# Block 3's first keys with their ones from DRAM, and batch 1's routing ahead of the first maxima, in a perceiver on one Trainium2 core

## The chip, the cores and the metric

The kernel runs on one core of one Trainium2 chip. The metric is the device time of one execution in microseconds, the median of several runs. Its engines are TensorE (PE for the products, PEld for the loading of its weights), VectorE (DVE), ScalarE (ACT), GpSimd (POOL) and SyncE (SP), which issues all DMAs of this kernel. Each engine works through its own instructions in their order; an instruction waits until the semaphores it names have been raised.

## What is computed

Two batches of 256 tokens of width 256 go through four blocks. Each block attends to a context of 4096 tokens (`xattn`), then to itself (`attn`), and ends with a feed-forward layer (`ffn`). What the change touches lies in blocks 2 and 3 (shortened from the reference):

```
x = x + L2_attn(layernorm(x))            # 16 heads
x = x + L2_ffn(layernorm(x))             # router over 8 experts, the best two
                                         # weighted, plus one shared expert
x = x + L3_xattn(layernorm(x), ctx, mask)  # 16 heads of 16, 4096 keys
x = x + L3_attn(...); x = x + L3_ffn(...)
```

In `L2_ffn` the logits of the router go to eight experts; the two largest get the gates softmax(v1, v2), all others zero. In `L3_xattn` scores are q·k / 4 plus a large negative number where the mask drops a key, then softmax over the 4096 keys, then the values.

## The kernel before

**Lanes and order.** Two lanes of work, `a` and `x`, share the engines, each with its own pools. The program is written in stages; a scheduler at build time then fixes the order of instructions on each engine from its own estimate of durations. Only what is chained by hand (`tie` for TensorE's instructions in block 3's exponents, `behind` for one instruction after another) is not free for it to move. All DMAs are on one queue, SP's, and use eight semaphores in turn: a DMA is issued only when the eighth before it has landed.

**Block 2, end.** The two batches are staggered: while batch 0's `l2_ffn` runs on lane a, batch 1's cross-attention and then `l2_attn(1)` run on lane x. `l2_attn` writes its queries to DRAM and loads them back as stacked tiles (`stack`, L526; the last of these loads is a `rows_from`). Its result is added at L1234. `l2_ffn(1)` follows on lane a: layernorm (statistics L426 and L427, a 128x2 step on VectorE L432, the power on GpSimd L417, `axn` L441), four transposes (L449), the plain copy `xf` (L468), logits (L1073, bias L1078), two rounds of `first_max` (L1089 to L1097) and some small steps that give the gates `g8` (to L1262). `along` (L1107 on) transposes the gates (L1111), halves them into `grow` (L1113), writes the 8 rows to DRAM and loads them back spread over 128 partitions (L1115, L1119). Then come the shared expert and four pairs of experts, each by `glu`: 12 + 12 products (L413), tanh on ACT (L1028), L1032, the gate on GpSimd (L1134), u (L1132 or L1135), and the split of u into a high part (ACT, L404) and a low part (VectorE, L407). Weights are split in the same way: loaded as `awr` (L340), high part `aw` on ACT (L404), low part on GpSimd (L406) or VectorE (L407). The sum x is written at L1269.

**Block 3's cross-attention.** `l3_xattn` is a generator for both batches. Its work is cut into 32 places: 2 batches x 4 groups of 4 heads x 4 pieces of 1024 keys. For each place there are two passes. `max_steps` loads the key tile (two DMAs from `akh_d`, one from `akl_d`, L1370; the mask row L1371, 16 KB) and, at a group's first piece, the query tile (six DMAs of 16 rows, L526), multiplies (L1378, two products of 64x512) and takes maxima (L1380, 128x1024 to 128x2, eight a place). `exponents` multiplies again with keys as the stationary side (L1407), takes exponentials (ACT, L1411; L1409 in the last places, where they are wide) and multiplies with the values (L581). The maxima run five places ahead of the exponents (`ahead`), so 40 reduces and one more come before the first exponent; afterwards one reduce stands beside each step of exponents. There are seven key tiles in a ring and three query tiles. A key tile holds, beside the three rows of each key element, a row of ones in which the first is the mask; `x3_tiles` fills each of the seven tiles with ones on GpSimd (L1300) and copies `unmask` into each of the three query tiles (L1296, GpSimd too). `later` holds steps that are due a number of exponent steps from now.

**Queries of block 3.** `x3_queries(b, x)` is a layernorm, transposes, a product with `x3.wq` and a write to `q_d` (L521). In `af` it follows `l2_ffn(b)`. For batch 1 its products use the PSUM banks ("mm" of lane a) which the first exponents need as score banks.

**Masks.** `masks`, in block 1, writes the mask numbers `md` and `mk_d` and a small tensor of ones, `fill_d`.

In the profile, `xf<-xk,xq` are the products for the maxima, `xpm<-xf` the reduces, `amm` or `xs<-xq,xk` the score products, `xp` the exponentials, `axn` the layernorm's output on lane a, `aqT` the queries of block 3.

Of the kernel before, what the change touches and what calls it, by code (L numbers as in the profile page):

```python
# [18 lines left out]
F32 = mybir.dt.float32  # L19
F32R = mybir.dt.float32r  # L20
# [8 lines left out]
P = 128  # L29
# [261 lines left out]
class Lane:  # L291
# [231 lines left out]
    def rows_from(self, x, at, n, src, step=1):  # L523

        to = x[at : at + step * (n - 1) + 1 : step].bitcast(F32)
        self.nc.sync.dma_start(to, src.bitcast(F32) if src.dtype == F32R else src)  # L526

# [116 lines left out]
class Perceiver:  # L644
# [461 lines left out]
    def along(self, fp, g):  # L1106
# [13 lines left out]
        return out  # L1120

    def glu(self, fp, h, wg, wu, xT, m, gate=None):


        k, nc = self.a, self.nc
        psg = k.proj_t(wg, xT, m)
        g = k.t(fp, [P, 2, S], "g")
        self.tanh_half(g, psg)
        psu = k.proj_t(wu, xT, m)
        u = k.t(fp, [P, 2, S], "u")  # L1130
        if gate is None:
            nc.vector.scalar_tensor_tensor(u, psu, 0.5, g, ALU.mult, ALU.mult)  # L1132
        else:
            nc.gpsimd.tensor_tensor(g, g, gate, ALU.mult)  # L1134
            nc.vector.tensor_mul(u, psu, g)  # L1135
        k.split(h, u)
# [36 lines left out]
    def l2_attn(self, k, b, x):  # L1173
# [3 lines left out]
        with k.pool("a2", bufs=1) as ap:  # L1177
# [37 lines left out]
            for g in range(4):  # L1215
                k4, q4 = ks[g % 2], qs[g % 2]
                g4 = slice(GRP * g, GRP * g + GRP)
                k.stack(k4, q_d, g4, k.KEYS)
                k.stack(q4, q_d, g4, k.QUERIES)
                k.rows_from(q4, k.ADD, 2, sqd[:, g4, :])  # L1220
                k.rows_from(k4, k.ADD + 2, 2, sqd[:, g4, :])
                acc = k.mm()
                ps = [k.mh_scores(ap, lambda j: k4[:, j, t * P : (t + 1) * P], lambda j: q4[:, j, :], 0.5) for t in range(2)]
                for t in range(2):
                    k.mh_values(ps[t], lambda j: v[:, t, 4 * g + j, :], acc, t == 0, t == 1)
                k.mh_finish(g, acc, o)()
# [10 lines left out]
    def l2_ffn(self, b, x):  # L1237
# [4 lines left out]
        with k.pool("f2", bufs=2) as fp:  # L1242
            br = k.row("f2.br", fp)
            xf = k.t(fp, [P, 2, S], "xf", bufs=1)
            xnT = k.transposed(k.layernorm(x, fp), fp, "xnT", plain=xf)
            lg = self.logits(k, xf, "f2.gate", bias=br)
            v1, hot1 = self.first_max(lg, "a")
            v2, hot2 = self.first_max(self.without(lg, hot1), "b")
# [13 lines left out]
            nc.vector.tensor_add(g8, g8, h2)  # L1262
            gates = self.along(fp, g8)
            h = k.t2(fp, [P, 10, S], "h", bufs=1)
            self.glu(fp, h[:, 0:2, :], s1, s3, xnT, 0)
            for e in range(0, 8, 2):
# [17 lines left out]
    def x3_tiles(self, at):  # L1284
# [8 lines left out]
        if c == 0 and i < self.Q_SETS:  # L1293

            x = tile(f"q{i}", S)
            nc.gpsimd.tensor_copy(x, self.unmask.unsqueeze(1).to_broadcast([P, GRP, S]))  # L1296
            self.x3_q.append(x)
        if at < self.RING:
            x = tile(f"k{at}", 512)
            nc.gpsimd.memset(x.bitcast(F32), 1.0)  # L1300
            self.x3_k.append(x)
        return self.x3_q[i % self.Q_SETS], self.x3_k[at % self.RING]
# [10 lines left out]
    def masks(self):  # L1313

        k, nc = self.a, self.nc
        with k.pool("mask", bufs=1) as mp:
# [10 lines left out]
            nc.sync.dma_start(self.fill_d, fill)  # L1327

    def x3_queries(self, b, x):

        k = self.a
        (wq,) = k.weights("x3.wq")
        with k.pool("x3q", bufs=1) as ap:
            xnT = k.transposed(k.layernorm(x, ap), ap, "xnT")
            k.to_dram(k.proj_t_split(wq, xnT, ap, "qT", bias="x3.bq"), self.q_d[b])

    def l3_xattn(self, xs):
# [8 lines left out]
        def place(at):  # L1346
# [3 lines left out]
            return b, g, c, i  # L1350

        def max_steps(at):


            b, g, c, i = place(at)
            g4 = slice(GRP * g, GRP * g + GRP)
            q4, k4 = self.x3_tiles(at)
            if c == 0:
                for h in range(2):
                    at = h * self.HALF  # L1360
                    for r, part in enumerate(k.QUERIES):
                        src = self.q_d[b, part].rearrange("m (h d) n -> d (m h) n", d=HD)
                        k.rows_from(q4, at + r, HD, src[:, g4, :], self.PARTS)
                    if i >= self.Q_SETS:
                        k.rows_from(q4, at + self.SHIFT, 2, self.zeros, self.PARTS)
                state[i] = q4, k.t(self.early, [P, 2, GRP, 2 * n_c], "pm", bufs=2), []
            q4, pm, ks = state[i]
            u2 = slice(2 * c, 2 * c + 2)
            for r, src in ((0, self.kh_d), (1, self.kh_d), (2, self.kl_d)):
                nc.sync.dma_start(k4[r :: self.PARTS].bitcast(F32), src[b, u2, :, g4, :].rearrange("u d j n -> (u d) j n"))  # L1370
            nc.sync.dma_start(k4[self.MASK :: self.HALF].bitcast(F32), self.mk_d[b, u2])  # L1371
            ks.append(k4)
            for j in range(GRP):
                for t in range(2):
                    both = self.x3_find()
                    for h in range(2):
                        rows = slice(h * self.HALF, (h + 1) * self.HALF)
                        tie(nc.tensor.matmul(both[:, h * 512 : (h + 1) * 512], lhsT=q4[rows, j, t * P : (t + 1) * P], rhs=k4[rows, j, :], start=True, stop=True))  # L1378
                    at = pm[:, t, j, 2 * c : 2 * c + 2]
# [82 lines left out]
        self.zeros = k.t(self.early, [2 * GRP, S], "zeros", F32R, bufs=1)  # L1462
        nc.gpsimd.memset(self.zeros.bitcast(F32), 0.0)
        xp = self.late
        self.x3_banks(k)
# [5 lines left out]
        yield 1, None  # L1471
        for at in range(ahead):
            steps = max_steps(at)
            advance(self.STEPS)
# [3 lines left out]
        self.tied = None  # L1478
        tie = self.tie
        for at in range(n):  # L1480
            steps = max_steps(at + ahead) if at + ahead < n else iter(())
            for s in range(4):
# [355 lines left out]
    def run(self):  # L1838
# [14 lines left out]
        nc.vector.tensor_mul(self.w12, self.w1h, a.col("f0.w2", 0, 8))  # L1853
        self.q_d = a.dram([B, 2, 2, P, S], "q_d")

# [4 lines left out]
        self.mk_d = a.dram([B, L // 512, GRP, 512], "mk_d")  # L1860
        self.v_d = a.dram([B, 4, P, L // 512, 4 * GRP * (HD + 1)], "v_d")
        self.md = a.dram([B, L], "md")

        self.fill_d = a.dram([4, 2048], "fill_d")
        
        def af(n, b):
# [3 lines left out]
            else:  # L1870
                xb[b] = self.l2_ffn(b, xb[b])
                self.x3_queries(b, xb[b])

        a.p_bufs = 2
        x.p_bufs, x.score_tags = 4, [(x, "s")]
        with ExitStack() as wa:
            a.wraw = wa.enter_context(a.pool("wraw", bufs=2))
            a.wp = wa.enter_context(a.pool("w", bufs=4))
            with ExitStack() as early:
# [3 lines left out]
                with self.psum(x, mm=2, s=2, pr=1), self.psum(a, mm=3), x.pool("wraw", bufs=1) as x.wraw, x.pool("w", bufs=2) as wp, x.pool("xq", bufs=1) as self.xq:  # L1883
# [17 lines left out]
                    with x.pool("x", bufs=1) as xp:  # L1901
# [4 lines left out]
                        for n in range(1, 3):  # L1906
# [5 lines left out]
                            if n == 2:  # L1912
                                self.early = early.enter_context(a.pool("x3e", bufs=2))
                            xb[1] = self.xattn(xp, n, 1, xb[1], xq[1])
                            self.prep_alone(xp, *self.ALONE.get((n, 1), (0, ())))
                            if n < 2:
# [3 lines left out]
                    x.mm_tags = ["mm", "mm", "pr"]  # L1920
                    xb[1] = self.l2_attn(x, 1, xb[1])
                x.p_bufs = 3
                with ExitStack() as self.x3_psum, self.psum(a, mm=2, acc=1), x.pool("x3", bufs=2) as self.late:
# [50 lines left out]
```

## Time and profile before

| | |
|---|---|
| median of 3 runs | 1514.52 us (1509.82, 1514.52, 1514.57) |
| the profiled execution | 1513.83 us |
| its span, first to last instruction | 1512.1 us |
| granted TensorE clock, mean over the span | 0.94 |
| busy in the span: PE, DVE, ACT, POOL | 89%, 73%, 59%, 34% |
| end of `l2_attn(1)`: x of batch 1 written | 863.8 us |
| first maximum (L1380) begins | 870.44 us |
| gates transposed and halved (`grow`) | 904.03 us |
| `l2_ffn(1)` writes x (L1269) | 940.84 us |
| first score products of the exponents flow | 954.92 us |
| last maximum ends | about 1231.5 us |
| last value products of block 3's cross-attention | 1275.5 us |
| PE busy in 850–900, 980–1000 us | 30.19 of 50, 19.82 of 20 |

Times in the profile are microseconds from the start of the span. A timeline's line gives the start, the length, the engine, the line of the program, the operation, the output and inputs, and in brackets the idle time before it and what ended it. A group's line gives the busy time and the mean length in ns of one instruction, and after the bar the idle time just before them. "PEclk" or "clock" is the share of TensorE's full clock that was granted.

### The profile page before, as it was taken

Reading aid. Unit: us, or ns where it says so; the run is one execution under the profiler, and the core shown is the slowest. Engines: PE = TensorE matmul, PEld = TensorE weight load, DVE = VectorE, ACT = ScalarE, POOL = GpSimd, SP = SyncE. Lnnn points to the kernel's source line nnn. Section 1 sums busy time; section 2 is a strip of 40 time slices with the busy share of each in tenths; the row PEclk is TensorE's granted clock in tenths of the full one; section 3 lists DMA queues with packets and bytes.
Section 4 is the critical chain, followed back from the end, with each engine's and each line's share of the span. In section 5 each row is a group of like instructions: output and inputs, shape, how many; then the busy total and the mean of one; then the engine's idle time right before and its main releaser. Section 6 shows DMA issues by size and latency. Waiting matters only on the chain.

```text
span 1512.1 us, 29306 instructions
## 1 busy us (share of the span) xinstructions
PE 1353.1 (89%) x11278; PEld 1108.8 (73%) x11278; DVE 1108.8 (73%) x1863; ACT 891.4 (59%) x1644; POOL 521.0 (34%) x397
## 2 busy tenths in 40 slices
PE   7898788979998999998998767899999998987698
PEld 6898778969998998998898436455555544774588
DVE  6999855446467878885588599799999961566675
ACT  6676555637775655764664303688888897233243
POOL 6755344335445544664335413000000001531130
PEclk9999999979999999999999959899999999986799
DMA  8754164556455556445642542333333312300262
GB/s 288 250 152 131 33 190 161 184 172 217 149 177 169 176 177 214 146 155 179 164 128 89 172 165 95 121 119 109 126 122 107 113 53 61 136 1 30 84 218 75
DMA packets 125143, 212.00 MB, mean 140 GB/s; under 512 B 12840, under 2 KB 89240, under 8 KB 121480
## 3 DMA queue, kind: packets, MB, share of 16 engines
q1 hardware_dynamic: 125004, 210.13, 44.1%
q8 instruction: 89, 1.46, 0.4%
q14 instruction: 50, 0.41, 0.1%
HBM read 181.32 MB, written 28.61 MB: 139 GB/s over the span
## 4 chain that ended last, share of the span: by engine, by line
PE 48%; DVE 14%; ACT 5%; DMA 4%; POOL 4%; issue 3%; SPq 1%; POOLq 0%; DVEq 0%; ACTq 0%
PE amm L413 9%; PE xacc L581 7%; PE xmm L413 6%; PE xf L1378 5%; DVE xpm L1380 4%; PE xs L413 4%; PE xpr L413 4%; DMA awr<-in_w 2%; PE amm L1407 2%; POOL aw L406 2%; ACT xp L1409 1%; PE xmm L788 1%; PE amm L1796 1%; PE xs L1407 1%; PE amm L581 1%
## 5 line engine op out<-in xcount | busy, mean ns | idle before, releaser
L1380 DVE TENSOR_REDUCE xpm<-xf 128x2 f32<-128x1024 f32 x256 | 310.2, 1234 | 7.5 <-PE xf L1378 5.9
L1411 ACT ACTIVATE xp<-amm 128x512 f32<-128x512 f32 x284 | 162.0, 595 | 29.6 <-PE amm L1407 17.6
L406 POOL TENSOR_TENSOR aw<-awr,aw 128x1024 fp32r<-128x1024 f32 (+1 forms) x53 | 126.5, 2389 | 148.2 <-ACT aw L404 114.8
L404 ACT CAST aw<-awr 128x1024 fp32r<-128x1024 f32 (+1 forms) x112 | 114.0, 1021 | 99.8 <-DMA awr<-in_w 60.3
L413 PE MATMUL xmm<-xvx,xpT 128*128 128x256 f32 x1152 | 167.2, 291 | 2.8 <-DVE xo L801 1.3
L581 PE MATMUL xacc<-xp,xv 128*17 128x256 f32 x2048 | 161.0, 387 | 4.1 <-DVE xot L1430 1.1
L413 PE MATMUL xs<-xkx,xqkT 128*128 128x256 f32 x1152 | 162.1, 285 | 2.7 <-POOL xkx L738 1.9
L738 POOL TENSOR_TENSOR xvx<-xraw,xvx 128x512 fp32r<-128x512 f32 x96 | 131.9, 1389 | 89.6 <-ACT xvx L736 89.1
L1378 PE MATMUL xf<-xk,xq 64*128 64x512 f32 x512 | 135.8, 527 | 22.2 <-DVE xpm L1380 13.6
L413 PEld LDWEIGHTS xmm<-xvx,xpT 128*128 128x128 f32 x1152 | 147.9, 193 | 6.0 <-DVE xo L804 2.0
L413 PEld LDWEIGHTS xs<-xkx,xqkT 128*128 128x128 f32 x1152 | 147.6, 191 | 4.6 <-POOL xkx L738 2.1
L1378 PEld LDWEIGHTS xf<-xk,xq 64*128 64x128 f32 x512 | 51.1, 196 | 124.1 <-issue 83.2
L407 DVE TENSOR_TENSOR aw<-awr,aw 128x1024 fp32r<-128x1024 f32 (+1 forms) x59 | 86.6, 1473 | 60.9 <-ACT aw L404 60.8
L1445 POOL TENSOR_TENSOR ax<-xou,xmh_ri 128x128 f32<-128x128 f32 x8 | 3.2, 402 | 315.9 <-DVE xmh_ri L1441 315.9
L413 PE MATMUL amm<-axnT,aw 128*128 128x256 f32 x636 | 98.9, 313 | 10.2 <-ACT axnT L404 5.5
L413 PE MATMUL amm<-ah,aw 128*128 128x256 f32 x768 | 99.6, 286 | 6.0 <-ACT au L1013 2.9
L413 PEld LDWEIGHTS amm<-axnT,aw 128*128 128x128 f32 x636 | 91.3, 217 | 17.8 <-ACT axnT L404 7.2
L413 PEld LDWEIGHTS amm<-ah,aw 128*128 128x128 f32 x768 | 94.7, 191 | 8.7 <-POOL aw L406 3.7
L738 POOL TENSOR_TENSOR xkx<-xraw,xkx 128x512 fp32r<-128x512 f32 x48 | 72.1, 1503 | 82.9 <-ACT xkx L736 82.3
L1411 ACT ACTIVATE xp<-xs 128x512 f32<-128x512 f32 x148 | 88.0, 595 | 11.3 <-PE amm L1407 7.8
L1407 PE MATMUL amm<-xq,xk 64*128 64x256 f32 x568 | 89.3, 283 | 3.0 <-DVE aqT L402 2.7
L777 ACT ACTIVATE xp<-xs,xnm 128x512 f32<-128x512 f32 x96 | 66.2, 690 | 34.8 <-DVE xnm L771 32.6
(603 smaller groups left out, 2920.6 us busy)
## 6 DMA issues: line engine op xcount, KB each, us to landing
awr<-in_w SPq DMA_DIRECT2D x105, 512.0 KB
xraw<-in_ctxT SPq DMA_DIRECT2D x108, 256.0 KB
xraw<-in_ctx SPq DMA_DIRECT2D x96, 256.0 KB
xk<-akh_d SPq DMA_DIRECT2D x64, 256.0 KB
av_d<-xkvv SPq DMA_DIRECT2D x16, 544.0 KB
xv<-av_d SPq DMA_DIRECT2D x32, 272.0 KB
akh_d<-xkvk SPq DMA_DIRECT2D x32, 256.0 KB
akl_d<-xkvk SPq DMA_DIRECT2D x32, 256.0 KB
```

Of the source, the lines that this page charges most:

```text
L404: nc.scalar.copy(dst.h, src)
L406: return lo.tensor_tensor(dst.l, src, dst.h.bitcast(F32), ALU.subtract)
L407: return nc.vector.tensor_sub(dst.l, src, dst.h)
L413: tie(self.nc.tensor.matmul(out, lhsT=x, rhs=y, start=start and i == 0, stop=stop and i == 2))
L581: inst = self.nc.tensor.matmul(acc[STRIP * j : STRIP * j + v(j).shape[1], :S], lhsT=v(j), rhs=p[:, j, :], start=start, stop=stop)
L738: nc.gpsimd.tensor_tensor(x.l, r, x.h.bitcast(F32), ALU.subtract)
L777: tie(nc.scalar.activation(p, score.pop(i), AF.Exp, bias=least[q], accum_out=su))
L788: tie(nc.tensor.transpose(pst[:, t * P : (t + 1) * P], p[:, t * P : (t + 1) * P], self.eye))
L1378: tie(nc.tensor.matmul(both[:, h * 512 : (h + 1) * 512], lhsT=q4[rows, j, t * P : (t + 1) * P], rhs=k4[rows, j, :], start=True, stop=True))
L1380: nc.vector.tensor_reduce(at, both.rearrange("p (h n) -> p h n", h=2), axis=AX.X, op=ALU.max)
L1407: tie(nc.tensor.matmul(ps[h][:, j, :], lhsT=ks[c][rows, a + j, s * P : (s + 1) * P], rhs=q4[rows, a + j, :], start=True, stop=True))
L1411: exps = [nc.scalar.activation(p[:, h, a : a + 2, :], ps[h], AF.Exp, scale=0.25) for h in range(2)]
```

## The change

It has six parts.

- Key tiles are no longer filled on GpSimd. The first seven loads of the ring bring the mask and the ones as a fourth DMA of 256 KB from a new tensor `mo_d`, which `first_masks` writes once; in the program it is called after block 2's cross-attention of batch 1. Later loads bring the 16 KB mask row as before. The query tiles' `unmask` is copied by ACT instead of GpSimd.
- `load_keys` is separated from `max_steps`. The first four key tiles (16 DMAs) are issued right after `l2_attn(1)`'s last stacked load.
- In `l2_ffn` of batch 1 the shared expert goes ahead of `first_max`, and the gates are spread by `along_here`: eight products with a broadcast column of the identity, and four copies on ACT, without DRAM. The first place's maximum products stand behind the last of these products (`self.gated`).
- `q_d` has a new layout. Its writes are four DMAs instead of one, and a query tile is loaded by three DMAs of 32 rows, whose source repeats 16 rows for the two halves of the tile, instead of six of 16 rows.
- `x3_queries` of batch 0 stands after `l2_attn(1)` in the program instead of after `l2_ffn(0)`.
- `x3_queries` of batch 1 is done in pieces inside the exponents, as `later` steps, in banks of the scores.

```diff
+    def along_here(self, fp, g):
...
+        for e in range(0, 8, 2):
+            ps = k.mm2()
+            for i in range(2):
+                self.gated = nc.tensor.matmul(ps[:, i, :], lhsT=self.eye[0:8, e + i : e + i + 1].to_broadcast([8, P]), rhs=row, start=True, stop=True)
+            nc.scalar.copy(out[:, e : e + 2, :], ps)
+        return out
...
-                k.rows_from(k4, k.ADD + 2, 2, sqd[:, g4, :])
+                self.stacked = k.rows_from(k4, k.ADD + 2, 2, sqd[:, g4, :])
...
+            last = b == B - 1
+            if last:
+                self.glu(fp, h[:, 0:2, :], s1, s3, xnT, 0)
             v1, hot1 = self.first_max(lg, "a")
...
-            gates = self.along(fp, g8)
...
+            if last:
+                gates = self.along_here(fp, g8)
...
-            nc.gpsimd.tensor_copy(x, self.unmask.unsqueeze(1).to_broadcast([P, GRP, S]))
+            nc.scalar.copy(x, self.unmask.unsqueeze(1).to_broadcast([P, GRP, S]))
...
-            x = tile(f"k{at}", 512)
-            nc.gpsimd.memset(x.bitcast(F32), 1.0)
-            self.x3_k.append(x)
+            self.x3_k.append(tile(f"k{at}", 512))
...
+    def first_masks(self):
+
+        nc, n_u = self.nc, 2 * self.N_C
+        nc.sync.dma_start(self.mo_d[:, 0], self.md[:1, : n_u * 512].rearrange("a (u n) -> (a u) n", n=512).unsqueeze(1).to_broadcast([n_u, GRP, 512]))
+        ones = self.fill_d[:1, :].unsqueeze(1).to_broadcast([n_u, HD - 1, GRP * 512])
+        nc.sync.dma_start(self.mo_d[:, 1:].rearrange("u d j n -> u d (j n)"), ones)
...
+    def x3_queries_steps(self, b, x, tie):
...
+            xn = k.layernorm(x, ap)
+            yield 4
+            xnT = k.t2(ap, [P, 2, S], "xnT")
+            ps = bank().rearrange("p (a n) -> p a n", a=2)
...
+            for m in range(2):
+                yield 3
+                ps = bank()[:, :S]
...
+        def load_keys(at):
...
+            if at < self.RING:
+                loads.append(nc.sync.dma_start(k4[self.MASK :: self.PARTS].bitcast(F32), self.mo_d[u2].rearrange("u d j n -> (u d) (j n)")))
+            else:
+                nc.sync.dma_start(k4[self.MASK :: self.HALF].bitcast(F32), self.mk_d[b, u2])
+            if at < n_c:
+
+                for x in loads:
+                    k.behind(x, self.stacked)
...
+                for r, part in enumerate(k.QUERIES):
+                    src = self.q_d[b, part, :, g4, :].unsqueeze(0).to_broadcast([2, HD, GRP, S])
+                    nc.sync.dma_start(q4[r :: self.PARTS].bitcast(F32), src)
...
+                        if b == g == c == 0:
+
+                            k.behind(inst, self.gated)
...
+        queries = self.x3_queries_steps(1, xs[1], tie)
...
+        later.append([6, asked])
         for at in range(n):
-            steps = max_steps(at + ahead) if at + ahead < n else iter(())
+            if at + ahead < n:
+                load_keys(at + ahead)
+                steps = max_steps(at + ahead)
...
-                self.x3_queries(b, xb[b])
...
+                            if n == 2:
+                                self.first_masks()
...
                     xb[1] = self.l2_attn(x, 1, xb[1])
+                    self.x3_queries(0, xb[0])
+                    next(l3)
```

Built, the order of instructions on the engines is this around the change. On SP the 16 key loads follow `l2_attn(1)`'s stacks and batch 0's four query writes; then come two weights, the query tile q0, k4, q1, k5, values, k6, values, q2 and, amid q2, the weights of the experts' second half (`w2`). The two writes of `mo_d` stand on SP at the place of 467 us in the profile of before, between a value write and context loads. On VectorE the low part of `w2` stands between the seventh and eighth reduce. On ACT one copy of `unmask` stands before `l2_attn(1)`'s first exponent. The first exponent still follows the 41st maximum product on TensorE. The scheduled place of `x3_queries(0)`, inside `l2_attn(1)`, stays nearly the same.

## The prediction, made before the change was run

> **What bounds the kernel now.** I read the groups of the page first, then window tables around the change, then timelines of POOL, VectorE and TensorE from 837 to 980 us, then the DMA rows of 460–480 us, where the change puts a new write.
>
> ```profile
> span 1512.1 us, 29306 instructions
> ...
> L1380 DVE TENSOR_REDUCE xpm<-xf 128x2 f32<-128x1024 f32 x256 | 310.2, 1234 | 7.5 <-PE xf L1378 5.9
> ...
> L1378 PE MATMUL xf<-xk,xq 64*128 64x512 f32 x512 | 135.8, 527 | 22.2 <-DVE xpm L1380 13.6
> ```
>
> Block 3's 256 maxima are VectorE's largest group, and products and reduces wait for each other. From 980 to 1230 us both engines are full, so the stage can only start earlier, not run faster. Around its start:
>
> ```profile
> 940.00:960.00 20.00, 10.51 (x53) 6.95 (x52) 10.12 (x16) 8.28 (x13) 5.40 (x3) 0.71 0.44 133
> 960.00:980.00 20.00, 20.00 (x220) 10.54 (x218) 18.81 (x16) 16.65 (x31) 0.00 (x0) 0.94 0.30 96
> ```
>
> (window; busy us of PE, PEld, DVE, ACT, POOL; clock; DMA share; GB/s.) Half of 940–960 us is idle on both: that is the room. Its beginning is on POOL (start, length):
>
> ```profile
> 858.98 7.03 POOL L1300 MEMSET xk<- 128x2048 f32 x4
> ...
> 867.45 5.28 POOL L1300 MEMSET xk<- 128x2048 f32 x3
> 872.69 1.03 POOL L1296 CAST xq<-ac_unmask 128x1024 fp32r<-128x1024 f32 x1
> 873.82 0.70 POOL L417 TENSOR_TENSOR abn_rs<-abn_ve,amhalf 128x2 f32<-128x2 f32 x1
> ```
>
> Batch 1's layernorm (L417) stands behind the fills, and on VectorE its 128x2 step runs as long as they do, against 0.17 us at 944.98:
>
> ```profile
> 864.83 8.91 DVE L432 TENSOR_SCALAR abn_ve<-abn_mv 128x2 f32<-128x2 f32 x1
> 870.44 3.31 DVE L1380 TENSOR_REDUCE xpm<-xf 128x2 f32<-128x1024 f32 x2
> ```
>
> Its end is on TensorE:
>
> ```profile
> 946.48 1.18 PE L449 MATMUL amm<-ac_eye,axn 128*128 128x128 f32 x4 [5.67 <-issue]
> 948.33 3.44 PE L413 MATMUL amm<-axnT,aw 128*128 128x256 f32 x12 [0.67 <-ACT axnT L404]
> 951.70 0.51 PE L1407 MATMUL amm<-xq,xk 64*128 64x256 f32 x1
> 954.92 0.50 PE L1407 MATMUL amm<-xq,xk 64*128 64x256 f32 x3 [2.71 <-DVE aqT L402]
> ```
>
> Exponents wait for x3_queries(1), which holds their PSUM banks. 41 reduces are done at 938.72, the 42nd starts at 955.79.
>
> **The change, part by part.**
>
> *1. Fills, routing, gates, maxima (one chain).* x of batch 1 is ready at 863.8 + 0.7 = 864.5. With no fill ahead: statistics 1.2 (the rows from 943.99), power 0.8, axn 0.8, four cold transposes 1.2, copy 0.6, logits 1.9, bias 0.2: 871.2. Routing's 17 small steps, 0.2 each where alone (888.57–889.18) and some 0.3 with engine changes: 4.7; transposes 1.1; grow (L1113) 0.6: **877.6**, against 904.03. The shared expert's 24 products (2.91 for 12, cold) run beside routing. Eight gate products follow: fp32 over 256 columns take 0.52 in L1195's rows, 1.04 at half clock, with four ACT copies between: some 4.5, so the first reduce comes at 882.5, not 870.44.
>
> From grow, VectorE must do 41 reduces (1.14 start to start: 46.7), weight lows (4 x 1.4), four experts (L1032, u, ah: 0.62 each, 8.1 with the shared ah), x (0.7), statistics and axn (1.9), shift rows (0.8): 63.8. In 904–941.6 the same mix left 37.6 - 32.74 = 4.9 idle. 877.6 + 63.8 + 4.9 = 946.3 for the 42nd reduce, not 955.79: **-9.5**. Bounds: -12 if the experts' waits close, -5 if the gate products run cold and routing waits more. The removed gate round trip (three DMAs, 904.46 to about 908) hid beside the shared products and is worth nothing more.
>
> *2. Queries loaded by 3 DMAs of 32 rows instead of 6 of 16.* No such form is in the trace: the source is cut as 2 x 16 rows (the two halves of the tile read the same), the target as 32. Fewer issues (3 x 0.6 us of SP a group). SP carries, in order: four key tiles, q0, k4, q1, k5, values, k6, values, q2, and amid q2 the weights w2 of the second expert half. VectorE's low part of w2 now stands between reduces 7 and 8, at about 892 (877.6 + 12.5 of work + 2 idle); all later reduces are queued behind it. Before w2 stand seven 128 KB query loads (0.9 MB) and some 4.3 MB of other data. At the fullest rate seen (353 GB/s at 467 us) that is 15 us, but in parallel with their issue from 864.5, so w2 lands by 885: cost **0**. The other end, from the row where DMAs are cut in few outer parts:
>
> ```profile
> DMA  8646899989956263446445546635455697499985
> GB/s 321 219 171 184 232 280 239 218 300 321 287 143 157 82 137 123 150 164 198 164 171 184 212 178 205 157 130 191 177 218 198 212 294 212 171 266 335 335 246 198
> ```
>
> (474–480 us in 40 slices.) Here the key writes akh_d and akl_d, whose DRAM side is 8 x 16 rows, run at about half share and 130–210 GB/s. If eight outer parts give half of 350 GB/s, two give an eighth, 44: 3.0 us for one load, an estimate by proportion. Then 7 x 3.0 + 12.3 + 2 after 864.5: w2 lands at 900, its high part (ACT, 1.05) ends at 901.5, and VectorE stands 9.5. Meanwhile the experts' waits, the 4.9 above, pass unseen: net 4.6. The few-part row is the nearer one, so I take **+4.6**; range 0 to 9.5.
>
> The Trainium skill, page "DMA: Bandwidth & Descriptors", section "Why a DMA increments its semaphore by 16 and not by 1", says that a DMA uses as many engines, up to 16, as divide the slowest dimension of both sides, always the lowest-numbered ones. It speaks against this change: two engines for a query load. By it the sum below stands or rises by up to 4.9; by the full-rate row it falls by 4.6. No run here shows two engines yet.
>
> *3. Ones from DRAM.* The seven first tiles load 256 KB instead of 16 KB in a fourth DMA: 1 MB for the first four (3 us), early, beside l2_attn(1): hidden. But mo_d must be written: 0.98 MB, outer dimension 8, on SP at 467 us between value writes and context loads, where lane x lives off DMA:
>
> ```profile
> 480.81 0.62 ACT L736 CAST xkx<-xraw 128x512 fp32r<-128x512 f32 x1 [5.25 <-DMA xraw<-in_ctxT]
> ...
> 482.27 1.69 PE L413 MATMUL xpr<-xw,xkx 128*128 128x256 f32 x12 [2.67 <-ACT xkvv L386]
> ```
>
> At full rate 2.8 us, at the half rate of the row above 5.3; 468–471 us, where the share is 0.45 on average, can absorb some 1.6. And SP lets a DMA go only when the eighth before it has landed, so a slow write holds the context loads back. **+3.5**, range 0 to 5.6.
>
> *4. Query tiles copied by ACT.* One (1.03 on POOL) stands ahead of l2_attn(1)'s first exponent, which waits for it: **+0.7** (0 to 1). Two more sit behind that stage's last work: nothing.
>
> *5. Queries of batch 1 in pieces.* Four transposes (0.6) and twelve products (1.67 warm) move from the idle room into a stage where PE is at 20.00 of 20, with 1.65 of VectorE low parts and one weight low (1.23). Each piece holds a score bank through its low part (in the old place VectorE waited 3.31 for one). **+3.5**; range 2.3 to 8.
>
> *6. The rest.* Batch 0's queries stay, as scheduled, inside l2_attn(1); four writes instead of one stand ahead of the keys on SP. The scheduler shifts a few instructions in blocks 1 and 2: 0, range -3 to +3.
>
> Sum: -9.5 + 4.6 + 3.5 + 0.7 + 3.5 = **+2.8** on the profiled execution's 1513.83 (span 1512.1 and 1.73 around it): 1516.6. That run is 0.7 below the median of the three shown, 1514.52, so on the median 1517.3: **1517**. The rivals' times are on the median too.
>
> **Rivals.**
>
> *Faster.* Query loads run at full rate and the mask write finds room: -9.5 + 0.7 + 3.5 = -5.3: 1509. For it: DMA stands idle in 894–904 us. Against it: the half-share row.
>
> *Slower.* DMAs of few outer parts decide: w2 holds VectorE for all of 9.5, and mo_d costs 5.6: -9.5 + 9.5 + 5.6 + 0.7 + 3.5 = +9.8: 1524. Its place is the DMA queue, at 467 and at 865–900 us; it decides once its two prices pass 5.3 together, and tells by measurement from 9.8. Against it: w2's wait may hide behind expert work.
>
> *The start moves, the stage gives it back.* The pieces hold banks where no slack is: +8 for part 5, rest as summed: +7.3: 1522. Then the change doesn't do what its room promised. For it: PE 20.00 of 20; against it: each bank is held for some 2 us only.
>
> **Numbers.** 0.3% (4.5 us) is about what a measurement can tell. Forecast, no change that can be told: 0.42, 1517 (1512 to 1519). Faster 0.25; slower by few-part DMAs 0.22; slower by banks 0.11. Faster 0.25, same 0.41 and slower 0.34, a hundredth of the forecast lying beyond the bound. The range 1506 to 1524 takes in the faster case down to -8 (parts 2 and 3 at nothing, part 1 at -12) and the slower one to its centre.
>
> **What would show it.** Part 1: POOL's fills gone, the 128x2 step at 0.2 us, grow near 877.6, first reduce near 882.5, first exponents near 946. Part 2: VectorE idle before w2's low part near 892–901, released by awr. Part 3: ACT's wait near 480 longer than 5.25. Part 5: reduce-to-reduce gaps in the first 40 us of exponents. I am wrong if w2 lands before 890, if mo_d delays nothing, or if the exponents start later than 950 without a wait for w2.

## The result, and the profile after

The changed kernel takes 1522.3 us (median of 8 runs, 1516.14 to 1529.55) against 1514.55 for the kernel before on the same chip (8 runs, 1509.82 to 1518.32): ratio 1.0053, interval 1.0037 to 1.0070. That is slower, by a little more than the 0.3% that the prediction took as what a measurement can tell. The forecast was 1517, "no change", with 1506 to 1524 as its range: the time lies in the range, 5 us above the forecast, and beyond the 1512 to 1519 that "no change" had. The profiled execution took 1522.82 us (span 1521.0) against 1513.83 (1512.1): +8.99.

First the groups of the page after:

```profile
span 1521.0 us, 29318 instructions
...
L1454 DVE TENSOR_REDUCE xpm<-xf 128x2 f32<-128x1024 f32 x256 | 308.6, 1220 | 15.5 <-PE xf L1448 13.7
...
L1448 PE MATMUL xf<-xk,xq 64*128 64x512 f32 x512 | 135.2, 526 | 19.4 <-DVE xpm L1454 19.3
```

The work on the maxima is the same as before; what waits is not. VectorE now stands 13.7 us for products of maxima, 5.9 before. The window table of the same stretch (columns as before):

```profile
940.00:960.00 20.00, 13.90 (x36) 4.91 (x36) 19.96 (x22) 0.36 (x1) 0.00 (x0) 0.50 0.07 24
960.00:980.00 20.00, 19.71 (x164) 10.79 (x166) 15.70 (x16) 13.67 (x26) 0.00 (x0) 0.76 0.18 56
```

The room in 940–960 us, which VectorE used for 10.12 us of 20, is closed (19.96). But it is filled with maxima that come late (the clock granted to TensorE there is 0.50), and the exponents start at 960.81 instead of 954.92.

VectorE's timeline after shows the chain from x of batch 1 to the second weights:

```profile
872.15 0.17 DVE L432 TENSOR_SCALAR abn_ve<-abn_mv 128x2 f32<-128x2 f32 x1
...
882.52 0.40 DVE L1129 TENSOR_SCALAR agrow<-amm 8x256 f32<-8x256 f32 x1
...
889.58 2.36 DVE L1454 TENSOR_REDUCE xpm<-xf 128x2 f32<-128x1024 f32 x2 [4.76 <-PE xf L1448]
...
901.90 1.21 DVE L1454 TENSOR_REDUCE xpm<-xf 128x2 f32<-128x1024 f32 x1
907.94 1.22 DVE L407 TENSOR_TENSOR aw<-awr,aw 128x1024 fp32r<-128x1024 f32 x1 [4.83 <-ACT aw L404]
...
930.92 1.60 DVE L407 TENSOR_TENSOR aw<-awr,aw 128x1024 fp32r<-128x1024 f32 x1 [3.32 <-ACT aw L404]
```

The first line is the fix at work: the 128x2 step took 8.91 us beside the fills and takes 0.17. `grow` comes 11.41 us after x is done (871.11), where it took 40.24. Then the new losses: the first reduce waits 4.76 for the gate products, the weights of the second expert half (w2) hold VectorE 4.83, and later weights 3.32, where ACT's cast stood behind expert products that had come late.

A balance by stretches says where +8.9 of span came from. x is the end of the sum that `l2_attn(1)` writes; "exponents" is the time from which their first score products flow.

| stretch | before | after | difference |
|---|---|---|---|
| start of `l2_attn(1)` (its first scores) | 837.24 | 839.16 | +1.9 |
| of that: up to 460 us +0.9, the `mo_d` stretch to 490 us +4.2, from there -3.2 | | | |
| `l2_attn(1)`: first scores to x | 26.55 | 31.95 | +5.4 |
| x to `grow` | 40.24 | 11.41 | -28.8 |
| `grow` to exponents | 50.89 | 78.29 | +27.4 |
| exponents to last value products | 321.68 | 325.67 | +4.0 |
| from there to the end | 235.5 | 234.5 | -1.0 |

The two large rows belong together: maxima that ran before `grow` run behind it now. Their sum is -1.4. Starts of the same program move by some us from run to run (`l2_attn(1)` of a second profile of the changed kernel starts 6.2 later), so lengths of stretches are compared below, and the first line's parts only where an experiment repeats them.

### The profile page after: what moved, and what is told of

Same layout as the page of the kernel before. It is cut to its first block, busy times and chain, and to the rows that moved or that the text cites. A ratio compares the mean times of both kernels' runs of the same rounds, so it can differ in the third digit from the quotient of the medians.

```text
span 1521.0 us, 29318 instructions
## 1 busy us (share of the span) xinstructions
PE 1365.6 (90%) x11294; PEld 1117.1 (73%) x11294; DVE 1099.3 (72%) x1863; ACT 897.3 (59%) x1651; POOL 508.4 (33%) x387
## 4 chain that ended last, share of the span: by engine, by line
PE 56%; DVE 19%; DMA 10%; ACT 7%; issue 4%; POOL 3%; SPq 1%; DVEq 0%; ACTq 0%; POOLq 0%
PE amm L413 10%; PE xmm L413 9%; PE xacc L581 8%; PE xs L413 6%; PE xf L1448 5%; DVE xpm L1454 4%; DMA awr<-in_w 4%; PE xpr L413 4%; PE xmm L788 2%; PE amm L1481 2%; DVE aw L407 2%; POOL aw L406 2%; ACT aw L404 2%; ACT xp L1483 1%; PE amm L1885 1%
## 5 line engine op out<-in xcount | busy, mean ns | idle before, releaser
L1454 DVE TENSOR_REDUCE xpm<-xf 128x2 f32<-128x1024 f32 x256 | 308.6, 1220 | 15.5 <-PE xf L1448 13.7
L1485 ACT ACTIVATE xp<-amm 128x512 f32<-128x512 f32 x284 | 161.9, 595 | 33.6 <-PE amm L1481 22.1
```

Source lines behind the costliest of these rows:

```text
L1454: nc.vector.tensor_reduce(at, both.rearrange("p (h n) -> p h n", h=2), axis=AX.X, op=ALU.max)
L1485: exps = [nc.scalar.activation(p[:, h, a : a + 2, :], ps[h], AF.Exp, scale=0.25) for h in range(2)]
```

## The experiments

The theory after the result: the early start is worth what was predicted, and DMAs whose outer dimension is small take it back, the query loads at w2 and the ones at the context loads. The first rival: the start gives less. The second: the stage of the exponents gives it back. Ratios are to the kernel before on the same chip.

**Query loads of 16 rows.** The rest of the change stays, the new layout of `q_d` too.

```diff
-                for r, part in enumerate(k.QUERIES):
-                    src = self.q_d[b, part, :, g4, :].unsqueeze(0).to_broadcast([2, HD, GRP, S])
-                    nc.sync.dma_start(q4[r :: self.PARTS].bitcast(F32), src)
...
+                for h in range(2):
+                    for r, part in enumerate(k.QUERIES):
+                        k.rows_from(q4, h * self.HALF + r, HD, self.q_d[b, part, :, g4, :], self.PARTS)
```

> The changed kernel with only the query loads turned back to six DMAs of 16 rows; the order on all engines but SP stays the same. Theory: three DMAs whose source is cut as 2 x 16 rows run about 3 us each and hold the weights w2 back; VectorE's wait before w2's low part (4.83 us in the changed kernel) falls below 1 us, the exponents start 3 to 5 us earlier, and the time is 1.001 to 1.003 of before instead of 1.0053. Rival (w2 is late for another reason: the eight semaphores, or its weight buffer): the wait stays above 3 us and the time at 1.005.

Measured: 1516.65 (12 runs), ratio 1.0011 [0.9990, 1.0032]: 6 us better than the change. `grow` to exponents took 70.1 us, not 78.3. SP's timeline of the changed kernel, and then of this one, from the first query load to the issue of w2 (start, time until the last of the group is issued, count at the end):

```profile
871.27 1.68 SPq L1439 DMA_DIRECT2D xq<-aq_d  x3
...
875.49 6.55 SPq L1439 DMA_DIRECT2D xq<-aq_d  x3
884.91 1.13 SPq L1418 DMA_DIRECT2D xk<-akh_d  x2
...
890.29 3.21 SPq L1418 DMA_DIRECT2D xk<-akh_d  x2
...
898.68 0.33 SPq L340 DMA_DIRECT2D awr<-in_w  x1
```

```profile
866.95 4.54 SPq L526 DMA_DIRECT2D xq<-aq_d  x6
...
874.17 3.69 SPq L526 DMA_DIRECT2D xq<-aq_d  x6
877.91 1.23 SPq L1418 DMA_DIRECT2D xk<-akh_d  x2
...
881.13 0.38 SPq L340 DMA_DIRECT2D awr<-in_w  x1
```

w2 is issued 27.4 us after the first query load with few-part DMAs, 14.2 with twice as many of 16 rows. Not all of that difference is the shape of the loads: the scheduler also changed SP's order, and w2 now stands ahead of k6, its values and q2. The run with GpSimd's copies, further down, settles this: it has loads of 16 rows and w2 amid q2, as the changed kernel has it. Its SP timeline:

```profile
869.24 5.00 SPq L526 DMA_DIRECT2D xq<-aq_d  x6
...
889.96 0.33 SPq L340 DMA_DIRECT2D awr<-in_w  x1
```

w2 comes 20.7 us behind the first query load there, and VectorE's low part of it (903.20 us) waits for nothing. So at that place in the queue the shape alone is enough to remove the wait. How slow the loads are shows in the windows (the last two columns are the DMA share and GB/s), in the changed kernel between the loads of k4 and k5, and here while q2's loads are issued, behind k6 and its values:

```profile
879.00:886.00 7.00, 6.12 (x29) 5.28 (x29) 4.70 (x16) 3.52 (x6) 0.00 (x0) 0.74 0.13 50
```

```profile
886.00:890.00 4.00, 4.00 (x25) 3.87 (x23) 2.03 (x3) 0.60 (x1) 0.37 (x1) 0.62 0.97 360
```

A share of 0.13 is two sixteenths: two of the 16 DMA engines' worth. In the changed kernel's queue, SP stands 14.5 us for query loads to land (waited for, us in total, times, longest; 871 to 901 us); with 16 rows no such line is there up to the issue of w2.

```profile
SPq L1418 <- DMA xq<-aq_d: 9.5, 4, 2.9
SPq L1439 <- DMA xq<-aq_d: 5.0, 2, 3.1
```

SP issues nothing from 882.04 to 884.91: k5's first load is let go when the eighth DMA before it has landed, the third load of q0, which was issued by 872.95, some 12 us earlier. So the loss is more than the query loads' own transfers: slow loads hold the eight semaphores, and all that follows waits. VectorE in this kernel comes to w2 without a wait:

```profile
896.83 1.22 DVE L1453 TENSOR_REDUCE xpm<-xf 128x2 f32<-128x1024 f32 x1
897.97 1.22 DVE L407 TENSOR_TENSOR aw<-awr,aw 128x1024 fp32r<-128x1024 f32 x1
899.10 1.22 DVE L1453 TENSOR_REDUCE xpm<-xf 128x2 f32<-128x1024 f32 x1
```

**The ones written late.** `first_masks` keeps its writes, but they stand behind `l2_attn(0)`'s last stacked load, away from the context loads.

```diff
...
+        for x in (mask, fill):
+            self.a.behind(x, self.stacked)
```

> The changed kernel with only the two writes of the tensor of ones moved, behind block 2's last stacked load of batch 0; the order on all other engines stays the same. Theory: the write of 0.98 MB at 467 us delays the context loads; with it gone ACT's wait near 480 us falls from 8.03 back to about 5.2 us and TensorE's from 5.44 to 2.7, and 490 us is reached 4 us earlier; of these some 3 are made good again by 837 us in the changed kernel as it is, so the time falls by 1 to 4 us, to 1.0025 to 1.0045 of before. Rival (the wait has another cause, the order of SP): ACT's wait stays at 8.

Measured: 1517.63, ratio 1.0025 [1.0002, 1.0047], 4 us better than the change. ACT's wait in the context stretch is 3.34, less than the 5.25 of before. The wait at w2 stays, as its query loads do (6.48).

**The write of `mo_d` alone**, put into the kernel before, which then never reads it; and the same bytes with 15 outer parts instead of 8 in the write of ones. `first_masks` itself is otherwise that of the changed kernel.

```diff
+                            if n == 2:
+                                self.first_masks()
...
-        ones = self.fill_d[:1, :].unsqueeze(1).to_broadcast([n_u, HD - 1, GRP * 512])
-        nc.sync.dma_start(self.mo_d[:, 1:].rearrange("u d j n -> u d (j n)"), ones)
+        ones = self.fill_d[:1, :].unsqueeze(1).to_broadcast([HD - 1, n_u, GRP * 512])
+        nc.sync.dma_start(self.mo_d[:, 1:].rearrange("u d j n -> d u (j n)"), ones)
```

> The kernel before with only the two writes of the tensor of ones added, which nothing reads; the order on all engines but SP stays the same. Theory: ACT's wait near 480 us grows from 5.25 to about 8, 490 us comes 4 us later, and what is left at the end is 1 to 4 us: 1.001 to 1.003 of before. Rival A (later slack takes it all up): 1.000. Rival B (no delay at all): the wait stays 5.25.

> The kernel before with the unused write of ones added, with the same bytes, but its outer dimension of 15 rows instead of 8; the order on all engines but SP is the same as there. Theory (a DMA of few outer parts runs on few engines): the write takes 3 us instead of 5.5, and ACT's wait near 480 us, 8.03 with the outer dimension of 8 and 5.25 without the write, is 5.5 to 7; the time is 1.001 to 1.003 of before. Rival (the bytes, or the reads of one DRAM row by all, set it): 8 again and 1.0047.

Measured: 1521.31 (12 runs), ratio 1.0047 [1.0028, 1.0067] with 8 parts, and 1516.8, ratio 1.0005 [0.9986, 1.0024] with 15. By the medians the write alone costs about 6 us, more than the 1 to 4 expected, and with 15 parts nothing that can be told (-2 to +4). ACT's timeline around 484 us, of the changed kernel, of the write with 8 parts and of that with 15:

```profile
484.51 0.62 ACT L736 CAST xkx<-xraw 128x512 fp32r<-128x512 f32 x1 [8.03 <-DMA xraw<-in_ctxT]
```

```profile
485.62 0.62 ACT L736 CAST xkx<-xraw 128x512 fp32r<-128x512 f32 x1 [8.03 <-DMA xraw<-in_ctxT]
```

```profile
483.87 0.62 ACT L736 CAST xkx<-xraw 128x512 fp32r<-128x512 f32 x1 [5.90 <-DMA xraw<-in_ctxT]
```

ACT's wait falls by 2.1 us with 15 parts. The profiles are less sharp than the medians: from 460 us to the products that stand at 489.72 in the kernel before, 8 parts lose 4.0 us and 15 parts 1.9, and `l2_attn(1)` starts at 843.57 in both. So the outer parts decide a part of the price, 2 us in this stage, and the rest of the medians' difference is not traced. TensorE adds its own: in the changed kernel the products behind this wait run at half clock (granted clock 0.50).

```profile
485.97 2.93 PE L413 MATMUL xpr<-xw,xkx 128*128 128x256 f32 x12 [5.44 <-ACT xkvv L386]
```

They took 1.69 at full clock behind an idle time of 2.67 in the kernel before. With 15 parts they still take 2.93, behind 3.32.

**Both repairs** (query loads of 16 rows, ones late).

> The changed kernel with both: query loads as six DMAs of 16 rows, and the writes of ones behind block 2's last stacked load of batch 0; the order on all engines but SP stays the same. Theory (the two costs lie in different stages and add): 5.6 and 4.7 us less than the changed kernel's 1.0053, so 0.998 to 0.9995 of before; no wait above 2 us before w2's low part, ACT's wait near 480 at 3 to 5 us. Rival (they share their cost, since an earlier start only meets the next bound): 1.001 or above.

Measured: 1511.73 (12 runs, 1504.55 to 1514.64), ratio 0.9975 [0.9955, 0.9995]. The two costs add, within the intervals: 6.4 and 4.2 from the single repairs, 11.8 together (1.0053 less 0.9975, of 1515 us). Without its few-part DMAs the change is a small gain. x to exponents takes 82.2 us here, 91.1 before: -8.9.

**Batch 0's queries back in their place** (everything else as changed).

```diff
+                if b == 0:
+                    self.x3_queries(0, xb[0])
...
-                    self.x3_queries(0, xb[0])
```

> The changed kernel with only batch 0's block-3 queries back at their old place in the program, behind its feed-forward layer; the scheduler then orders some 500 instructions of TensorE otherwise. Theory: batch 1's attention in block 2 lasts 5.4 us longer in the changed kernel because ACT's casts of the query weights, which now land later, stand between its exponentials; it falls from 31.9 to some 27.5 us (0.9 stays, for the copy of the query tile), and the time by 3 to 5 us, to 1.002 to 1.0035. Rival (the key loads, now early, crowd that stage's loads): it stays at 31 us and above, and the time at 1.005.

Measured: 1532.41, ratio 1.0112 [1.0091, 1.0133]. It doesn't answer its question. The scheduler moved some 500 instructions on TensorE from block 1 on, and the kernel was already 7 us late at the context stretch, with the same wait there (8.00). Inside `l2_attn(1)` the waits for weights were gone, but ACT's copy of `unmask` had moved into the middle of the exponentials and waited for a query write:

```profile
865.35 1.04 ACT L1318 CAST xq<-ac_unmask 128x1024 fp32r<-128x1024 f32 x1 [2.98 <-DMA aq_d<-aqT]
```

**Query tiles copied by GpSimd again** (with both repairs).

```diff
-            nc.scalar.copy(x, self.unmask.unsqueeze(1).to_broadcast([P, GRP, S]))
+            nc.gpsimd.tensor_copy(x, self.unmask.unsqueeze(1).to_broadcast([P, GRP, S]))
```

> As the run with both repairs, and the three query tiles copied from the mask of ones on GpSimd again instead of ACT; the order of instructions changes only from batch 1's attention in block 2 on. Theory: the copy of 1.04 us no longer stands before that stage's first exponential, so the stage (31.9 us from the first scores to x in the changed kernel) is 1 us shorter and the time 0.5 to 1.5 us less than without this edit. Rival (the stage is long because ACT waits for weights): the stage stays within 0.5 us and so does the time.

Measured: 1515.16, ratio 1.0003 [0.9981, 1.0026], 3 to 4 us worse than with ACT's copy. `l2_attn(1)` did become 1.5 us shorter (27.51 against 29.02), as the copy's 1.04 suggests. But with that copy gone the scheduler put a weight cast on ACT ahead of the layernorm's:

```profile
873.83 1.04 ACT L404 CAST aw<-awr 128x1024 fp32r<-128x1024 f32 x1 [10.00 <-DMA awr<-in_w]
```

x to `grow` took 14.85 instead of 12.23. The edit's gain was lost to the order that came with it.

**Batch 1's queries in one go before the exponents** (with both repairs).

```diff
-        later.append([6, asked])
...
+                if b == 1:
+                    self.x3_queries(1, xb[1])
```

> As the run with both repairs, and batch 1's block-3 queries done in one go before the exponents again, as in the kernel before. Theory: the stage of exponents is 4 us shorter (321.7 instead of 325.3 from the first scores' flow to the last values), but the exponents start 8 to 11 us later, so the time is 4 to 7 us more than with the pieces. Rival (the pieces hold banks and cost as much as they save): the time is the same within 2 us or less.

Measured: 1513.18, ratio 0.9991 [0.9969, 1.0013]. The exponents' stage is 2.6 us shorter (322.9 against 325.5), and the way to it 5.7 longer from `grow` (75.7 against 70.0), 4.9 from x. The pieces are worth 1.5 us by the medians and 2 to 3 by the stretches, less than expected, and the difference of the ratios is inside their intervals.

**The gate of the first maxima.** Two ways to be rid of the 3.66 us that VectorE stands before the first reduce with both repairs: the maxima free to go before the gate products, or the gates through DRAM as before the change, with the maxima behind the gates' transposes.

```diff
-                        if b == g == c == 0:
-
-                            k.behind(inst, self.gated)
```

```diff
-            nc.tensor.transpose(ps[0:8, i * P : (i + 1) * P], g[:, i, :], self.eye)
+            self.gated = nc.tensor.transpose(ps[0:8, i * P : (i + 1) * P], g[:, i, :], self.eye)
...
-                gates = self.along_here(fp, g8)
+                gates = self.along(fp, g8)
```

> As the run with both repairs, but the first maximum products need not stand behind the gate products, so that they may mix with the routing; the order changes only from batch 1's routing on. Theory (VectorE's work bounds the way from x to the exponents): in the run with both repairs VectorE is idle some 12 of the 82.2 us from x to the first exponents, most of it before the first reduce at 883; reduces that start earlier fill that idle time, though each small routing step then waits for a reduce of 1.2 us, so the way is 4 to 8 us shorter and the time 0.992 to 0.995 of before. Rival (routing bounds it, as the change's order would have it): the gates come 10 us later, the experts with them, and the time is the same or up to 5 us more than with both repairs: 0.9975 to 1.001.

> As the run with both repairs, but batch 1's gates go out through DRAM again, with the first maximum products behind the two transposes of the gates. Theory: the eight gate products with four copies (5.8 us on TensorE at half clock, VectorE idle 3.7 before the first reduce) are gone, the DMA round trip of about 4 us lies beside the first reduces, and the exponents start 2 to 4 us earlier: 0.995 to 0.9965 of before. Rival (the gate DMAs wait behind key and query loads on SP's queue): the experts' first gate multiplication comes later than now, and the time is 2 us or more above the run with both repairs: 0.999 or more.

Measured: without the gate 1512.06 (12 runs), ratio 0.9989 [0.9963, 1.0016]: nothing gained, though the first reduce came 10.5 us behind x and not 18.2. The routing came later for it (`grow` 15.11 us after x, not 12.23), the first gated expert's step on VectorE by 4.3 us (26.4 behind x against 22.1), and from x to the exponents VectorE stood 14.1 us in all, where it stood 14.0 with both repairs. x to exponents was 81.8 against 82.2. The theory that the wait was worth its length fell.

With the gates through DRAM: 1504.98 (8 runs, 1497.63 to 1510.52), ratio 0.9959 [0.9937, 0.9982], the best version, faster than both kernels. Timelines of both repairs, and of both repairs with the gates through DRAM:

```profile
877.09 0.40 DVE L1129 TENSOR_SCALAR agrow<-amm 8x256 f32<-8x256 f32 x1
...
877.54 4.71 PE L1134 MATMUL amm<-agrow,ac_eye 8*128 8x256 f32 x16 [0.67 <-DVE agrow L1129]
...
883.04 2.36 DVE L1455 TENSOR_REDUCE xpm<-xf 128x2 f32<-128x1024 f32 x2 [3.66 <-PE xf L1449]
```

```profile
870.27 0.83 PE L1449 MATMUL xf<-xk,xq 64*128 64x512 f32 x4
870.49 0.40 DVE L1113 TENSOR_SCALAR agrow<-amm 8x256 f32<-8x256 f32 x1
870.89 2.35 DVE L1455 TENSOR_REDUCE xpm<-xf 128x2 f32<-128x1024 f32 x2
```

The 4.71 us of gate products stand between `grow` and the maxima; without them the reduce follows `grow` at once, and the round trip through DRAM lies beside maxima and expert products, though not wholly: VectorE stands 3.81 us at 881.66 for GpSimd's first multiplication by the gates. x to exponents took 78.8 us, against 82.2. Part of the better median is run-to-run movement: this profile's `l2_attn(1)` began 5 us earlier than the other's, and the intervals of the two ratios overlap. That it is faster than the kernel before is measured; that it beats both repairs alone rests on these stretches.

**The stage `l2_attn(1)`, twice more.** It was 31.95 us in two kernels with loads of 32 rows and about 29 in three with 16, with the same order of instructions.

> The changed kernel once more, unchanged, for one number: the length of l2_attn(1), from its first score products to the end of the sum that it writes. It was 31.95 us in the changed kernel's profile and 31.95 with the ones written late, both with query loads of 32 rows, and 28.79, 29.02 and 29.24 in three kernels with loads of 16 rows; the order of instructions in the stage is the same in all. In the two long ones TensorE's clock was lower in the stage. Theory (the drop goes with the program and not with chance): 31.5 to 32.5 again. Rival (the drop falls by chance on a run): 28.5 to 29.5. Query loads are issued only after this stage, so the theory would still lack a mechanism.

> The kernel with query loads of 16 rows once more, for the same number, 28.79 us in its first profile. Theory (the drop goes with the program): 28.5 to 29.5 again. Rival (chance): either length, and one of about 32 would refute the theory by itself. The rest is expected as before: no wait of VectorE above 2.5 us at the weights of the second expert half, grow to first exponents some 70 us against 78.

Measured, one execution each: the changed kernel again 1524.84 (before, beside it: 1518.01), its stage 28.46 us; loads of 16 rows again 1514.58, stage 29.50. The theory fell: the same program gives 31.95 and 28.46. The timelines of the changed kernel's two profiles (ACT's wait for weights, then TensorE's products with them) show what differs:

```profile
847.06 1.04 ACT L404 CAST aw<-awr 128x1024 fp32r<-128x1024 f32 x1 [2.14 <-DMA awr<-in_w]
...
848.64 0.39 PE L413 MATMUL amm<-axnT,aw 128*128 128x256 f32 x1 [1.94 <-ACT axnT L404]
...
850.18 2.66 PE L413 MATMUL amm<-axnT,aw 128*128 128x256 f32 x11
```

```profile
851.55 1.05 ACT L404 CAST aw<-awr 128x1024 fp32r<-128x1024 f32 x1 [0.47 <-DMA awr<-in_w]
...
853.14 0.39 PE L413 MATMUL amm<-axnT,aw 128*128 128x256 f32 x1 [0.27 <-ACT axnT L404]
...
854.68 1.58 PE L413 MATMUL amm<-axnT,aw 128*128 128x256 f32 x11
```

In the first, weights land later, TensorE stands 1.94 us, and its next eleven products take 2.66 us (granted clock 0.52); in the second it stands 0.27 and they take 1.58 (1.00). In the kernel before they take 1.57, and ACT waits for no weight in this stage: these weights, a pair with `x3.wq` in it, were issued at 836.01, 1.2 us ahead of the stage's first scores; now at 840.82, 1.7 behind them. Over nine profiles of the changed program or of those that differ from it only in parts that don't touch this stage, ACT's waits for weights are 1.9 to 2.7 us with stages of 28.4 to 29.5 in seven, and 3.5 and 4.0 with 31.95 in two. So the moved queries and the copy of `unmask` together cost this stage 1.9 us at least (27.51 without the copy on ACT, against 26.55 before: some 1.0 is the queries'), and 5.4 when the weights land late enough for the clock to fall. What decides a load's landing by a us or two is not settled.

## Why the prediction came out as it did

*1. Fills, routing, gates, maxima: -9.5.* Right, by size and by cause. With both repairs x to exponents is 82.2 us against 91.1: -8.9. The fills are gone and the 128x2 step takes 0.17. `grow` was put 13.1 us behind x and came 11.41 behind it; the first reduce was put 18.0 behind x and came 18.47. The gate products took 5.83 us (4.71 with both repairs), not 4.5. Two errors in the sum nearly cancel: from `grow` on VectorE worked 61.2 us with both repairs where the sum has 63.8, and stood 8.7 where it has 4.9. And x is complete at 863.79, so the start of 864.5 holds 0.7 too much, whether that is the length of the last addition or part 4's term, which the sum adds again; without it the sum would have been +2.1. That the removed round trip of the gates "is worth nothing more" was right, and the step stopped short of what follows: the products that replace it stand on the way, and with the round trip kept x to exponents is another 3.4 us shorter (78.8).

*2. Query loads in few parts: +4.6.* The mechanism was right, and so was the landing of w2: ACT starts on it at 906.86, 35.8 us behind x, where the sum had it land 35.5 behind. The size was not: 7.5 us in the profiles (89.7 against 82.2 from x to exponents), 6.4 by the medians. VectorE's idle time on this way shows where they lie: 21.0 us, against 14.0 with both repairs. 4.83 of it is at w2, where with 16 rows there is no wait; 1.5 more is at a later weight (3.32, of which 1.83 stay with 16 rows); 1.1 is before the first reduce (4.76 against 3.66), behind gate products of 5.83 us instead of 4.71. So that the net 4.6 meets the wait at w2 is luck. The sum had VectorE come to w2 27.5 us behind x and stand 9.5, and took off 4.9 for experts' waits that would "pass unseen"; VectorE came 32.0 behind x and stood 4.83. What the sum lacked is the later losses, some 2.6 us, which it put at nothing. The Trainium skill, page "DMA: Bandwidth & Descriptors", section "Why a DMA increments its semaphore by 16 and not by 1", puts such a load on two engines. The runs agree: the DMA share is 0.13 while query loads of 32 rows have the queue to themselves, and 16 rows instead of 32 made of 2 x 16 take the wait away, though they are twice as many DMAs.

*3. The write of the ones: +3.5.* Right in kind and near in size: +4.2 in the balance, 4.2 by the median of the kernel with late ones, and 6 by the median for the write alone in the kernel before (4.0 in its profile's stage). ACT's wait grew by 2.8 (8.03 against 5.25). The rest is the clock, which the sum didn't hold: twelve products 2.93 us instead of 1.69. The share of 468–471 us is 0.54 and not 0.45, which takes 0.2 from the 1.6 it was said to absorb.

*4. Query tiles copied by ACT: +0.7.* The copy takes 1.04 us ahead of the first exponent, as written; taking it away made the stage 1.5 shorter and lost more elsewhere by another order of casts.

*5. Queries in pieces: +3.5.* The stage of exponents became 4.0 us longer in the profiles, 2.6 against the kernel without pieces. But the term held only the cost. What goes out of the way to the exponents was counted in part 1, and measured it is 4.9 to 5.7: a net gain of 1.5 to 3. The rival that the stage gives it all back, +8, did not come, although its time, 1522, is the measured one. A time that fits is no proof of its case.

*6. The rest: 0.* This step failed most. "Batch 0's queries stay, as scheduled, inside l2_attn(1)" was true of the products, and was taken for true of the weight loads that go with them, which are issued about 3 us later against the stage. ACT's exponentials stand behind the casts of these weights. Parts 4 and 6 together were put at +0.7 and measured +1.9 to +5.4.

Set beside each other: -8.9, +7.5, +4.2, +5.4 (parts 4 and 6), +4.0, and -3.3 for what moved elsewhere (+0.9, -3.2, -1.0) make +8.9. The predicted sum was +2.8; of the 6.1 between, terms 2 and 4 with 6 account for 2.9 and 4.7, and the rest for -1.5. The terms as measured, without the 3.3 us gained elsewhere, make +12.2, beyond the range's upper end; that the range held the time is in part luck. The rival by few-part DMAs, 1524, had the right cause for the larger part of the loss.

## What to carry to other kernels

Before changing the shape of a DMA, look at the outer dimension of both its sides: fewer and larger DMAs with few outer parts can be slower, and hold back everything that follows in the queue. When a step is moved, follow its weight loads too, and see which engine's queue will stand behind their arrival. A stall that is removed is worth measuring together with the one that takes its place: here the gate products took back some 3 us of what the fills had cost, and the version without them and without the slow DMAs was the best, at 0.9959 of the kernel before.

## What the runs showed of the hardware

TensorE's clock falls at idle times with no one threshold: 12 products took 1.69 us (granted clock 1.00) behind an idle time of 2.67, and 2.93 (0.50) behind 3.32 (the 15-part write) and 5.44; in `l2_attn(1)`, with small gaps before, 11 products took 2.66 (0.52) behind 1.94 us, and 1.57 (1.00) behind 1.29 (the second profile with loads of 16 rows). The Trainium skill, page "TensorE: Matmul & The Clock Gate", section "Part 1: The HAM clock gate (the "warmup" mystery)", speaks of an idle window of about 3.4 us that runs freely. The drops behind 1.94 and 3.32 came earlier than a whole such window of idleness would have it. So a weight load that lands a little late costs more than its own delay: in the changed kernel's two profiles 1.6 us more of waiting for weights (3.50 against 1.88) came with 3.5 us more of the stage.
